# Position-biased attention in a four-layer network: query copies stored column by column, a preparation in smaller pieces, and a new order of the first loads and blocks

## The chip, the cores and the metric

The kernel runs on one core of a Trainium2 chip, in one launch. The metric is the time of one execution on the device, in microseconds; the kernel before has a median of 4787.96 us in three runs (4782.0 to 4789.18).

A core has these engines, named as the profile names them: PE (TensorE, matrix products; PEld is its load of the stationary operand), DVE (VectorE), ACT (ScalarE), POOL (GpSimd) and SP (SyncE, which here only issues DMAs). Each works through its own queue in order. Products land in PSUM (eight banks of 512 float32 on each of 128 partitions), all else lives in SBUF.

## The reference

The network has four layers on x of shape (2, 64, 64, 128): two images of 4096 tokens with 128 channels. Only layer 0 is touched by the change:

```python
# x = x + _L0_conv_ref(_gn(x), w_qkv, pos_emb_h, pos_emb_w)
qkv = jnp.einsum('bhwc,cd->bhwd', x, w_qkv)
q, k, v = jnp.split(qkv, [128, 256], axis=-1)      # 4 heads of 32, L = 4096 tokens
pos = relative_position_bias(q, pos_emb_h, pos_emb_w).reshape(B, nh, L, L)
scores = jnp.einsum('bnqd,bnkd->bnqk', q, k) * scale + pos
attn = jax.nn.softmax(scores, axis=-1)
out = jnp.einsum('bnqk,bnkd->bnqd', attn, v)
```

`_gn` is a group normalization over an image (32 groups of 4 channels). The bias `pos` of a query at (row, column) and a key at (row', column') is the query times an embedding of row' − row, plus the query times an embedding of column' − column. Layer 1 (a triangular product with gates), layer 2 (attention with squared scores, then a mixture of 64 experts) and layer 3 (attention, then a mixture of 8 experts) follow.

## The kernel before, in words

**Schedule.** The kernel is written with a tile framework: it gives every instruction a priority by its place in the program, and orders each engine's queue with a model of the times, so an instruction that is ready in that model can stand ahead of earlier ones that are not. Semaphores follow from the tiles. A pool gives each tag a number of buffers.

**Head of layer 0** (`Net.__init__`, `layer0`). Eight DMAs of 512 KB on SP's queue bring x into SBUF, four for each image. The weights (192 KB) and the two position tables (16 KB each) come on ACT's queue. Then the tables are transposed into `pe`, and a chain of small products (`gram`, `traces`, `tops`) makes bounds on the size of queries and keys. For each image, eight `group_block`s transpose 512 tokens at a time (line 113), take statistics (DVE, line 116) and copy the transposed block to `xT` (ACT, line 118); `group_stats` makes mean and scale of the groups; two instructions at line 395 normalize `xT` in halves. `lengths` squares `xT` (one half of each image on GpSimd, the other on ACT) and sums the squares by a product. From these `at_most` decides between `l0_bounded`, the path that is taken here, and a general one. The preparation of the first unit runs in between: 16 of its pieces ahead of that decision in the program, the rest behind it, and then the values of image 0 (`l0_values`).

**Main loop** (`l0_bounded`). A unit is one image, a pair of heads and half of the queries (2048): eight units. A unit has four blocks of 512 queries and, for each, 32 steps over 128 keys. In a step TensorE makes scores of both heads (line 615), ACT takes their exp (line 623), DVE multiplies by the column part `ew` of the bias, itself an exp (line 626), and TensorE adds up the weighted sum of the values two steps later (line 573). The row part of the bias is in the scores: the operands `qa` and `ka` carry it in 32 extra rows for each head. Eight units of 128 steps make 1024 steps.

**Preparation of a unit** (`l0_prepare`). It is a generator; the loop of the unit before takes one piece of it in every second step (64 slots a unit), ahead of which go the finishes of query blocks (`l0_finish`, three pieces each). Its parts are:
- queries: `projected` makes 2 x 512 of them in one PSUM tile; for each 512, `qa` gets 32 rows of either head by six copies on ACT and DVE (lines 677 to 687). Four of them also fill the rows that later hold the row bias with a copy of the queries, of which the column-bias products read every 64th, that is one column of the image;
- column bias: in each of four groups 16 products (`l0pw`, line 701) with a moving operand `qa[lo : lo + HD, :, y::S]`, for 32 columns y from row group 32 and for 32 from row group 96, into two PSUM tiles, partitions 0 to 63 of each; then two exps (line 712) write them to `ew`, and one DMA copies `ew` to the other 64 partitions;
- row bias: in each of four groups 16 products (`l0ph`, line 723) from row groups 0 and 64 into the two halves of one PSUM tile, and four copies (line 734);
- keys, where the half is the first: four pairs of 512 (`l0pk`) and 16 copies (lines 747, 748).

A float32 product takes two passes, so the profile counts two matmuls for each product in these lines.

## Time and profile before

| | |
|---|---|
| three runs | 4789.18, 4787.96, 4782.0 us |
| profiled execution | 4783.74 us, span 4781.9 us |
| mean granted TensorE clock | 0.963 |
| layer 0: head (to the first score product) | 0 to 87.4 us, PE busy 53.09 of its first 87 us, granted clock 0.80 |
| layer 0: main loop | 87 to 2088 us, PE busy 1962 of 2001, clock 1.00 |
| layer 1 and what follows | 2088 to 4782 us |

A line of the timeline gives the start and the length in us, engine, source line, operation, the tile written and those read, shapes and how many instructions were merged; in square brackets stands how long the engine was idle before and what ended that. A line of the waits gives who waited for whom, the total in us, how often, and the longest. A line of the chain gives start, length and what held the end at that time. Of merged matmuls the length reaches to the end of the last one, which overlaps the next group; distances between starts tell what TensorE spends.

### The profile page before, as it was taken

The numbers are of one execution on the slowest core, as the hardware profiler recorded it, in microseconds if no ns is written. First come the engines' busy times: TensorE is split into PE (matmuls) and PEld (weight loads), VectorE is DVE, ScalarE is ACT, GpSimd is POOL, SyncE is SP. The second block draws the span as 40 slices with busy tenths as digits, with TensorE's granted clock in tenths as the row PEclk, the third lists the DMA queues.
The fourth block names the chain that finished last, engine by engine and source line by source line (L and its number), as shares of the span: only waits on it lengthen the run. The fifth ranks groups of instructions, "written<-read, shape, count | busy, mean of one in ns | idle before, by whom it ended". The sixth has DMA issues, their size and how long they took to land.

```text
span 4781.9 us, 76270 instructions
## 1 busy us (share of the span) xinstructions
PE 4464.8 (93%) x32236; PEld 1739.6 (36%) x32236; DVE 2943.9 (62%) x4850; ACT 2697.7 (56%) x3157; POOL 945.6 (20%) x848
## 2 busy tenths in 40 slices
PE   6999999999999999977899999999967999999999
PEld 3333333333333333335323223222224444444444
DVE  5676767677766767766755657555554444444447
ACT  5666565656666665545666766676731443433326
POOL 1000000000000000004455555555521000000008
PEclk8999999999999999988999999999978999999999
DMA  1000000000000000000000000000034000000001
GB/s 47 10 1 10 1 10 1 10 1 1 10 1 10 1 13 1 1 5 21 6 1 1 1 1 1 1 1 1 1 109 181 1 0 0 0 1 0 0 1 36
DMA packets 42562, 60.16 MB, mean 13 GB/s; under 512 B 4224, under 2 KB 24928, under 8 KB 41568
## 3 DMA queue, kind: packets, MB, share of 16 engines
q1 hardware_dynamic: 40912, 54.34, 3.7%
q8 instruction: 257, 4.21, 0.4%
q10 hardware_dynamic: 1296, 0.82, 0.1%
q14 instruction: 97, 0.79, 0.1%
HBM read 42.56 MB, written 4.19 MB: 10 GB/s over the span
## 4 chain that ended last, share of the span: by engine, by line
PE 75%; DVE 11%; ACT 7%; issue 3%; POOL 2%; DMA 1%; SPq 0%; DVEq 0%; ACTq 0%; POOLq 0%
PE l0o L573 15%; PE l0sc L615 15%; PE scl L2126 9%; PE oTl L2085 9%; PE l2sc L1498 5%; PE l2pos L1245 5%; PE l2av L1544 3%; PE f3ex L2235 2%; DVE l2es L1518 2%; POOL l2es L1521 2%; ACT l0es L623 2%; ACT l2es L1529 1%; DVE l0es L626 1%; PE l0pw L701 1%; PE l1p L988 1%
## 5 line engine op out<-in xcount | busy, mean ns | idle before, releaser
L626 DVE TENSOR_TENSOR l0es<-l0es,l0qe 128x1024 f32<-128x1024 f32 x1024 | 1250.2, 1228 | 529.5 <-ACT l0es L623 528.4
L623 ACT ACTIVATE l0es<-l0sc 128x1024 f32<-128x1024 f32 x1024 | 1044.0, 1025 | 604.5 <-PE l0sc L615 599.5
L573 PE MATMUL l0o<-l0es,l0v 64*33 64x512 f32 x8192 | 1072.9, 592 | 32.2 <-DVE l0es L626 16.7
L615 PE MATMUL l0sc<-l0qe,ka 64*64 64x512 f32 x8192 | 1080.3, 595 | 5.7 <-ACT l0es L623 5.0
L1529 ACT ACTIVATE l2es<-l2es 128x1024 f32<-128x1024 f32 (+3 forms) x576 | 559.4, 984 | 264.8 <-POOL l2es L1521 257.7
L1521 POOL TENSOR_TENSOR l2es<-l2es 128x1024 f32<-128x1024 f32 (+3 forms) x352 | 581.2, 1662 | 493.6 <-DVE l2es L1518 424.9
L2093 DVE TENSOR_TENSOR accl<-accl,esl 128x1024 f32<-128x1024 f32 x240 | 302.5, 1261 | 424.6 <-ACT esl L2137 421.2
L1518 DVE TENSOR_SCALAR l2es<-l2sc 128x1024 f32<-128x1024 f32 (+3 forms) x320 | 338.8, 1059 | 312.1 <-PE l2sc L1498 311.5
L2137 ACT ACTIVATE esl<-scl 128x1024 f32<-128x1024 f32 x240 | 245.8, 1024 | 485.0 <-PE scl L2126 451.7
L615 PEld LDWEIGHTS l0sc<-l0qe,ka 64*64 64x64 f32 x8192 | 298.5, 133 | 568.0 <-issue 490.4
L573 PEld LDWEIGHTS l0o<-l0es,l0v 64*33 64x33 f32 x8192 | 255.5, 108 | 646.6 <-issue 518.7
L2126 PE MATMUL scl<-l3qT,l3kT 128*128 128x512 f32 x1024 | 487.3, 595 | 0.0
L1498 PE MATMUL l2sc<-l2q,kept 32*128 32x512 f32 (+3 forms) x2304 | 392.2, 624 | 86.2 <-ACT l2es L1509 62.2
L2085 PE MATMUL oTl<-esl,l3v 128*128 128x512 f32 x960 | 451.1, 592 | 0.0
L776 POOL TENSOR_TENSOR x<-x,l0y 128x256 f32<-128x256 f32 x32 | 23.4, 730 | 1994.5 <-DVE l0y L771 1899.8
L1544 PE MATMUL l2av<-l2es,kept 128*32 128x512 f32 (+3 forms) x2304 | 309.5, 588 | 0.0
L1245 PE MATMUL l2pos<-kept 128*32 128x512 f32 x2416 | 295.2, 597 | 0.1
L2085 PEld LDWEIGHTS oTl<-esl,l3v 128*128 128x128 f32 x960 | 181.7, 190 | 225.6 <-issue 221.8
L2126 PEld LDWEIGHTS scl<-l3qT,l3kT 128*128 128x128 f32 x1024 | 188.2, 191 | 207.5 <-issue 191.3
L1509 ACT ACTIVATE l2es<-l2sc 128x1024 f32<-128x1024 f32 x224 | 226.3, 1010 | 52.5 <-PE l2sc L1498 51.3
L1498 PEld LDWEIGHTS l2sc<-l2q,kept 32*128 32x128 f32 x2304 | 116.9, 188 | 329.4 <-ACT l2es L1509 163.5
L1245 PEld LDWEIGHTS l2pos<-kept 128*32 128x32 f32 x2416 | 78.1, 111 | 173.8 <-issue 173.0
(707 smaller groups left out, 3748.9 us busy)
## 6 DMA issues: line engine op xcount, KB each, us to landing
f2w<-in_L_ffn_weight_dram SPq DMA_DIRECT2D x32, 1024.0 KB, 13.1
l0qe<-l0qe SPq DMA_DIRECT2D x8, 1024.0 KB, 6.7
x<-in_x_dram SPq DMA_DIRECT2D x8, 512.0 KB, 8.8
out_dram<-x SPq DMA_DIRECT2D x16, 256.0 KB, 2.3
kept<-in_L_attn_pos_rev_dram SPq DMA_DIRECT2D x1, 1792.0 KB, 6.8
ew<-in_L_ffn_expert_w_dram SPq DMA_DIRECT2D x1, 512.0 KB, 4.1
kept<-in_L_attn_pos_rev_dram SPq DMA_DIRECT2D x1, 256.0 KB
f2b<-in_L_ffn_weight_dram ACTq DMA_DIRECT2D x2, 128.0 KB, 2.6
```

The lines of the kernel that those rows point to most:

```text
L573: nc.tensor.matmul(o[64 * h : 64 * h + HD + 1, r, :], lhsT=v1[rows, k, 2 * pair + h, :], rhs=es[rows, h, :], start=(k == 0), stop=(k == NC ...
L615: nc.tensor.matmul(sc[64 * c : 64 * c + 64, h, :], lhsT=ka[rows, k0 : k0 + 64], rhs=qa[rows, k // (NC // 2), qs], start=True, stop=True,)
L623: nc.scalar.activation(es, sc, AF.Exp)
L626: nc.vector.tensor_tensor(es, es, ew[:, :, qs], ALU.mult)
L1245: nc.tensor.matmul(out[part], lhsT=lhsT[:, part], rhs=rhs, start=start, stop=stop)
L1498: nc.tensor.matmul(sc[:, h2, off:], lhsT=kT[hs, k * P : (k + 1) * P], rhs=q[hs, off:], start=True, stop=True,)
L1518: nc.vector.tensor_scalar(es[:, :, lo:], sc[:, :, lo:], root, None, ALU.mult)
L1521: nc.gpsimd.tensor_tensor(part, part, part, ALU.mult)
L1529: nc.scalar.activation(es[:, :, off:], es[:, :, off:], AF.Silu)
L1544: nc.tensor.matmul(avs[i][hs, off:], lhsT=v[:, k, hs], rhs=es[h // 2][:, h % 2, off:], start=(k == 0), stop=last,)
L2085: nc.tensor.matmul(oT, lhsT=vs[b][:, k, :], rhs=es[:, i, :], start=(k == 0), stop=(k == NC - 1),)
L2126: nc.tensor.matmul(sc[:, i, :], lhsT=kTs[b][:, k * P : (k + 1) * P], rhs=qT[:, qb * 512 : (qb + 1) * 512], start=True, stop=True,)
```

## The change

- The position tables are loaded first on ACT's queue, then the weights, then blocks 4 and 5 of x (the first half of image 1); SP loads the other six.
- In the program the blocks and the normalization of image 0 and the blocks of image 1 now come first, then the tables and bounds, then image 1's normalization and the lengths; the whole preparation of the first unit comes behind the decision. Its PSUM tiles have a tag of their own (`first`, four buffers beside four of `misc`, in place of five).
- The square of the second half of image 1 is made on ACT and no longer on GpSimd.
- The queries for the column bias are written column by column, so that the 32 queries of a column lie together; the copies per 512 queries become eight, in three pieces.
- The column-bias products of both row groups go to the two halves of one PSUM tile.
- The two exps of a group, the two pairs of row-bias copies and the two pairs of key copies become pieces of their own.
- The copies of the values alternate between ACT and DVE.

The diff, cut to its core:

```diff
@@ __init__
-        src = ins["x"].rearrange("b h w c -> (b h w) c").rearrange("(g p) c -> p g c", p=P)
-        for g in range(0, B * NC, 8):
-            nc.sync.dma_start(out=self.x[:, g : g + 8, :], in_=src[:, g : g + 8, :])
+        self.load_x(nc.sync, [0, 1, 2, 3, 6, 7])
...
+    def load_x(self, queue, blocks):
+        src = self.ins["x"].rearrange("b h w c -> (b h w) c").rearrange("(g p) c -> p g c", p=P)
+        for g in blocks:
+            blk = slice(8 * g, 8 * g + 8)
+            queue.dma_start(out=self.x[:, blk, :], in_=src[:, blk, :])
@@ layer0
+            raw = wp.tile([2 * S - 1, 2, HD], F32, tag="raw", name="l0raw")
+            for i, n in enumerate("hw"):
+                nc.scalar.dma_start(out=raw[:, i, :], in_=ins[f"L0_conv_pos_emb_{n}"])
             nc.scalar.dma_start(out=w, in_=ins["L0_conv_w_qkv"])
+            self.load_x(nc.scalar, [4, 5])
...
-                tc.tile_pool(reuse_waits="tile", name="l0sp", bufs=5, space=PSUM) as ps,
+                tc.tile_pool(reuse_waits="tile", name="l0sp", bufs=4, space=PSUM) as ps,
             ):
+                def blocks(b):
+                    for g in range(NC // 4):
+                        self.group_block(ps, gst[:, b], b, g, xT[:, b, :])
+
+                def normed(b):
+                    gm, gr = self.group_stats(ps, gst[:, b], b)
+                    for half in range(2):
+                        part = xT[:, b, half * 2048 : (half + 1) * 2048]
+                        nc.vector.tensor_scalar(part, part, gm, gr, ALU.subtract, ALU.mult)
+
+                blocks(0)
+                normed(0)
+                blocks(1)
...
-                made = {}
-                first = self.l0_prepare(
-                    ps, (0, 0, 0), xT, w, pe, [ka], (qe[:, 0], qe[:, 1]), made
-                )
...
-                    if half:
+                    if half and b == 0:
                         nc.gpsimd.tensor_tensor(sq, part, part, ALU.mult)
...
-                for b in range(B):
-                    for g in range(NC // 4):
-                        self.group_block(ps, gst[:, b], b, g, xT[:, b, :])
-                    gm, gr = self.group_stats(ps, gst[:, b], b)
-                    for half in range(2):
-                        part = xT[:, b, half * 2048 : (half + 1) * 2048]
-                        nc.vector.tensor_scalar(part, part, gm, gr, ALU.subtract, ALU.mult)
+                normed(1)
                 for b in range(B):
                     for half in range(2):
-                        pieces(4)
                         lengths(b, half)
...
-                for _ in first:
+                for _ in self.l0_prepare(
+                    ps, (0, 0, 0), xT, w, pe, [ka], (qe[:, 0], qe[:, 1]), {}, tag="first"
+                ):
                     pass
-                self.l0_values(ps, 0, xT, w, v)
+                self.l0_values(ps, 0, xT, w, v, tag="first")
@@ l0_values
-            nc.scalar.copy(
+            (nc.vector.tensor_copy if g % 2 else nc.scalar.copy)(
@@ l0_prepare
-                left = [
-                    v.rearrange("p (x y) -> p x y", y=S)[:, :, : S // 2]
-                    for v in (qa[32:64, 0, cols], p0)
-                ]
                 yield
-                nc.scalar.copy(qa[:64, 1, cols], pq[64 * i : 64 * i + 64])
-                nc.vector.tensor_copy(qa[:HD, 0, cols], p0)
+                nc.scalar.copy(qa[:HD, 0, cols], p0)
+                nc.vector.tensor_copy(qa[64 : 64 + HD, 0, cols], p1)
                 yield
-                nc.vector.tensor_copy(left[0], left[1])
-                for h, p in ((0, p0), (1, p1)):
-                    right = [
-                        v.rearrange("p (x y) -> p x y", y=S)[:, :, S // 2 :]
-                        for v in (qa[96:128, h, cols], p)
-                    ]
-                    (nc.scalar.copy if h else nc.vector.tensor_copy)(right[0], right[1])
-                nc.scalar.copy(
-                    qa[64 : 64 + HD, :, cols], p1.unsqueeze(1).broadcast_to([HD, 2, 512])
-                )
+                nc.scalar.copy(qa[64 : 64 + HD, 1, cols], p1)
+                nc.vector.tensor_copy(qa[:HD, 1, cols], p0)
+                yield
+                for j in range(2):
+                    rows = slice(32 + 64 * j, 64 + 64 * j)
+                    for h, p, copy in ((0, p0, nc.scalar.copy), (1, p1, nc.vector.tensor_copy)):
+                        dst = qa[rows, h, : H2 // 2].rearrange("p (y x) -> p x y", y=S // 2)
+                        src = p.rearrange("p (x y) -> p x y", y=S)
+                        x = slice(8 * (g + i), 8 * (g + i) + 8)
+                        copy(dst[:, x, :], src[:, :, 32 * j : 32 * j + 32])
             yield
...
-            pw = [
-                ps.tile([P, 8, 2, S // 2], F32, tag="misc", name=f"l0pw{t}_{g}_{i}")
-                for i in range(2)
-            ]
+            pw = ps.tile([P, 8, 2, S // 2], F32, tag=tag, name=f"l0pw{t}_{g}")
...
-                        pw[i][:S, n, :, :],
+                        pw[64 * i : 64 * i + S, n, :, :],
                         lhsT=pe[lo : lo + HD, 1, S - 1 - y : 2 * S - 1 - y],
-                        rhs=qa[lo : lo + HD, :, y::S],
+                        rhs=qa[lo : lo + HD, :, (8 * g + n) * 32 : (8 * g + n + 1) * 32],
...
             for i in range(2):
+                if i:
+                    yield
                 y = 32 * i + 8 * g
                 dst = ew[:S].rearrange("p h (x y) -> p y h x", y=S)
-                nc.scalar.activation(dst[:, y : y + 8], pw[i][:S], AF.Exp)
+                nc.scalar.activation(dst[:, y : y + 8], pw[64 * i : 64 * i + S], AF.Exp)
...
             for lo in (0, 64):
+                if lo:
+                    yield
                 for kh, copy in ((0, nc.scalar.copy), (1, nc.vector.tensor_copy)):
...
                 pk = projected(1, g, f"l0pk{b}_{pair}_{g}")
-                yield
                 for i in range(2):
+                    yield
```

## The prediction

> **What bounds the kernel now.** I read the page first (shares, chain), then layer 0's stretches, its TensorE timeline, TensorE's waits, and the order of work in the first 90 us.
>
> ```profile
> span 4781.9 us, 76270 instructions
> PE 4464.8 (93%) x32236; PEld 1739.6 (36%) x32236; DVE 2943.9 (62%) x4850; ACT 2697.7 (56%) x3157; POOL 945.6 (20%) x848
> PE l0o L573 15%; PE l0sc L615 15%; PE scl L2126 9%; PE oTl L2085 9%; PE l2sc L1498 5%; PE l2pos L1245 5%; PE l2av L1544 3%; PE f3ex L2235 2%; DVE l2es L1518 2%; POOL l2es L1521 2%; ACT l0es L623 2%; ACT l2es L1529 1%; DVE l0es L626 1%; PE l0pw L701 1%; PE l1p L988 1%
> ```
>
> TensorE sets the end. Layer 0 runs from 0 to 2088 us: a head until the first score product at 87.41, then 1024 steps. Only layer 0 is edited, so the question is what TensorE does besides the steps, and how long the head is. TensorE's timeline in unit 0 shows the price of side work:
>
> ```profile
> 131.89 1.04 PE L573 MATMUL l0o<-l0es,l0v 64*33 64x512 f32 x8
> 132.86 1.98 PE L701 MATMUL l0pw<-l0qe,l0pe 32*64 32x64 f32 x32
> 134.76 1.09 PE L615 MATMUL l0sc<-l0qe,ka 64*64 64x512 f32 x8
> ...
> 178.32 1.04 PE L615 MATMUL l0sc<-l0qe,ka 64*64 64x512 f32 x8
> 179.18 1.04 PE L573 MATMUL l0o<-l0es,l0v 64*33 64x512 f32 x8
> 180.14 1.15 PE L723 MATMUL l0ph<-l0qe,l0pe 32*64 32x64 f32 x32
> 181.22 1.09 PE L615 MATMUL l0sc<-l0qe,ka 64*64 64x512 f32 x8
> ```
>
> The first column is the start. Groups of eight follow each other at 0.86 us (178.32 to 179.18), so a step is 1.72 us. A column-bias group (l0pw) holds TensorE from 131.89 + 0.86 = 132.75 to 134.76, 2.01 us; a row-bias group (l0ph), as many products of the same shape, from 180.04 to 181.22, 1.18 us.
>
> TensorE's waits from 90 to 2250 us, and one place behind the largest:
>
> ```profile
> PE l0o L573 <- DVE l0es L626: 16.7, 35, 2.3
> PE l0sc L615 <- ACT l0es L623: 5.0, 16, 1.9
> ```
> ```profile
> 352.06 0.58 ACT L677 COPY l0qe<-l0pq 64x512 f32<-64x512 f32 x1
> 352.66 1.02 ACT L623 ACTIVATE l0es<-l0sc 128x1024 f32<-128x1024 f32 x1
> 352.67 0.68 DVE L678 COPY l0qe<-l0pq 32x512 f32<-32x512 f32 x1 [0.81 <-ACT l0qe L677]
> ...
> 354.67 1.00 ACT L687 COPY l0qe<-l0pq 32x1024 f32<-32x1024 f32 x1
> 355.55 1.06 PE L573 MATMUL l0o<-l0es,l0v 64*33 64x512 f32 x8 [0.72 <-DVE l0es L626]
> ```
>
> The copies of queries sit ahead of exps and multiplications in the in-order queues, and the weighted sum comes late. Taking TensorE's groups from 352.65 to 358.03 against 0.86 each, this place loses 1.94 us. There are 14 such places (two in each of the seven units prepared in the loop); the same subtraction sums to 27.9 us.
>
> In the chain, the head starts like this:
>
> ```profile
> 1.94 11.20 DMA l0raw<-in_L_conv_pos_emb_w_dram
> 18.50 1.06 PE gt L113 x4
> 25.63 0.38 DVE gmv L125
> 34.03 1.81 DVE gst L116 x3
> 38.79 1.90 PE l0pq L657 x4
> 53.03 2.78 PE l0pw L701 x32
> ```
>
> TensorE's queue begins with the position table's transposes, which wait for a small DMA until 13.19; x's transposes queue behind and start at 18.43, when most of x has landed. The first query product stands behind image 1's statistics, at 38.72.
>
> **Column-bias products.** Before, the moving operand has a stride of 64 elements, and both row groups write the same 64 columns; after, it has runs of 32, and the groups write separate halves. L723's row has neither old trait: runs of 64, separate halves, 217 ns a product against 283 for L701. So I take 1.18 us: 2.01 − 1.18 = 0.83 us, 28 groups in the loop, 23.2 us, all on TensorE and so on the path. Bounds: 0 (both traits harmless, the weight load being the price: 148 ns against 133) and 25. The four groups in the head run at a granted clock of 0.50, where 64 pw products took 3.79 us and 122 ph ones 6.72: 59 against 55 ns, 0.5 us in all. One PSUM tile in place of two lets the next group start while the first is read; no wait on that shows today, so nothing.
>
> A page speaks against this edit: the Trainium skill, "PSUM — Partial Sum Buffer", section "PSUM bank collisions raise a hardware error", says that different row tiles cannot access one PSUM bank at the same time, and the new l0pw does just that. By it the pairs would not overlap, and the 23.2 us would be nothing. But l0ph puts row groups 0 and 64 into one tile's two halves and runs at 1.18 us: the row decides.
>
> **Query copies.** Of one 512-column block ACT did 0.58 + 0.36 + 1.00 = 1.95 us and DVE 0.68 + 0.42 + 0.42 = 1.52. After: each two copies of 512 (0.58; 0.69) and two of 256 whose writes step by 32 elements. ACT's strided exp (L712, 64x512 with step 64) takes 1.064 against 0.582 for the plain copy of that shape, 0.94 ns more an element, so ACT's 256 cost 0.36 to 0.60. On DVE the nearest strided row is L1058, 1.03 against 0.69 for 512, so 0.42 to 0.60. I take the strided ends: ACT 2.35, DVE 2.57 us a block; over 32 blocks (four a unit) that is 13 us more on ACT and 34 on DVE. Both engines have room: a step of 1.72 us holds 1.03 of exp and 1.23 of multiplication. What matters is how long one piece holds a queue. ACT's longest falls from 1.36 in a row (L686, L687) to about 1.2 with DVE turns between, in three pieces in place of two. The nearest row for such alternating pairs is L734 (0.58 on ACT, then 0.69 on DVE, twice a piece): around 180 to 186 TensorE loses nothing. Against it: ready pieces are pulled together (350.64 to 354.67), and DVE's 0.69 exceeds its free 0.49. So of 27.9 us lost I take 15 as regained, with bounds of −15 (losses half as large again) and 27.9 (as at L734).
>
> **The other pieces.** The exps of a group and the row-bias copies become two pieces each, the keys' copies too. Pieces per unit rise from 22 or 26 to 34 or 42; with about 12 of the finishes that is 54 at most of 64 slots, so none is left for the unit's end. They also put the SBUF copy on SP's queue later, with nothing behind it. PSUM copies of values alternate ACT (0.59) and DVE (0.69), while TensorE's 0.92 a group sets the pace: nothing.
>
> **Head.** Two loads of x move from SP's queue to ACT's, behind tables and weights. SP issued eight in 14.44 us, so two cost ACT's queue about 3.6 us; it has nothing else to do then, since x's first block must land. SP's later small loads start earlier and nobody waits. At 222 GB/s, with ACT's 1.2 MB sharing the engines, image 0 (2 MB) has landed by about (2 + 1.2) MB / 222 GB/s = 14.5 us, and TensorE now transposes block by block. Add two statistics (1.4) and today's path from aggregation to normalization (25.63 to 31.45, 5.8) and the first half of the normalization (1.3): query products at 23.0 in place of 38.7. From there to the first score is 87.4 − 38.7 = 48.7 us today. Into this falls more of image 1's work, and a square goes from GpSimd (3.60) to ACT (1.91); out go two table loads for a square root between exps (63.42, 65.69: 2.6 us), since no exp is issued that early any more. ACT was busy about 33 of those 48.7 us and TensorE about 35, so there are gaps to fill, and the second set of four PSUM tiles lets the preparation fill them. I take 46: first score at 69, a gain of 18. Bounds: 7, if image 1's statistics, normalization and copies (about 11 us) all lie on the path; 25, if copies fill ACT's gaps (23 + 39 us of ACT work).
>
> **Sum.** 23 + 0.5 + 15 + 18 = 56 us. The profiled execution took 4783.74 (span 4781.9, 1.8 around it), so 4727; the median of the runs is 4.2 higher, so I say 4731.
>
> **Rivals.**
> (a) Products and head gain, the copies' stalls stay, because pieces are pulled together again: 4788 − 42 = 4746. For it: 350.64 to 354.67.
> (b) Head gains nothing, because ACT, with its two loads, late copies and third square, sets its end: 4788 − 38 = 4750. For it: ACT's 8.64 busy of 10 us at 60 to 70; against: 5.68 and 6.62 in the windows before that.
> (c) The new layout does not do what it says, l0pw stays near 2 us: 4788 − 33 = 4755. For it: the weight loads; against: L723.
> (d) Slower. The alternation blocks both queues: eight hand-offs a block, DVE's copy waiting for ACT's and ACT's next for DVE's, each with exp or multiplication queued behind it and TensorE behind those. A place holds two blocks, 9.8 us of both engines' copies, of which 2.0 reach TensorE now. At 7 us it loses 14 × 5 = 70 more and the total is 4788 − 42 + 70 = 4816; it outweighs the products and the head from 2.0 + 42 / 14 = 5 us a place. For it: DVE waited for L677 27 times, 14.4 us; against: L734.
>
> **How the numbers follow.** Forecast 0.50 (4731; by its bounds from 4710, all at their best with 25 + 28 + 25, to 4753, with 23 + 5 + 7, below which it is one of the others), (a) 0.22, (b) 0.10, (c) 0.08, (d) 0.10. Reaching over (a), (b) and (c) and most of the forecast: 4706 to 4764. Runs of this kernel tell some 0.2% (9.6 us) from no change. Of (d)'s chance a little ends within that: faster 0.85, same 0.05, slower 0.10.
>
> **What would show it.** Right: l0pw's groups at about 1.2 us on TensorE, its matmul median near 217 ns; the first score product near 69 us and x's transposes from about 6; the wait of L573 for DVE's l0es well under 16.7 us. Wrong: l0pw still near 283 ns (c); a first score past 82 (b); waits for l0es above 25 us (a, then d). Outside layer 0 every stage should keep its length; a difference there would refute the working.

## The result: slower, and where the time went

The changed kernel took 4817.38 us in the median of four runs (4815.22 to 4823.44) beside 4787.91 for the kernel before: a ratio of 1.0066 with a 95% interval of 1.0049 to 1.0083. The forecast was 4731 with a range up to 4764. The profiled execution has a span of 4813.4 us, 31.5 more than before.

From the page of the changed kernel: the span, the engines' busy time, and the chain by line:

```profile
span 4813.4 us, 76320 instructions
PE 4468.1 (93%) x32236; PEld 1714.6 (36%) x32236; DVE 2984.2 (62%) x4890; ACT 2713.0 (56%) x3182; POOL 942.0 (20%) x847
PE l0o L577 15%; PE l0sc L619 15%; PE scl L2127 9%; PE oTl L2086 9%; PE l2sc L1499 5%; PE l2pos L1246 5%; PE l2av L1545 3%; PE f3ex L2236 2%; DVE l0es L630 2%; ACT l0es L627 2%; DVE l2es L1519 2%; POOL l2es L1522 2%; ACT l2es L1530 1%; PE l1p L989 1%; ACT l2es L1510 1%
```

TensorE still sets the end, and the column-bias products (1% of the chain before) are gone from this list. DVE's multiplications rose from 1% to 2%; ACT's exps stay at 2%. TensorE's waits from 90 to 2250 us (engine, line, what it waited for: us in total, times, longest) say which of the two holds it back:

```profile
PE l0sc L619 <- ACT l0es L627: 43.1, 26, 2.5
PE l0o L577 <- DVE l0es L630: 16.3, 26, 2.3
```

The second line is as before (16.7). The first was 5.0. The score products wait for a PSUM tile that the exp has not read yet, and the exp is late. The timeline of the changed kernel at the place that the prediction showed (start, us, engine, line):

```profile
349.74 1.02 ACT L627 ACTIVATE l0es<-l0sc 128x1024 f32<-128x1024 f32 x1
349.75 0.68 DVE L681 COPY l0qe<-l0pq 32x512 f32<-32x512 f32 x1 [0.64 <-ACT l0qe L680]
350.79 0.61 ACT L689 COPY l0qe<-l0pq 32x256 f32<-32x256 f32 x1
350.80 1.23 DVE L630 TENSOR_TENSOR l0es<-l0es,l0qe 128x1024 f32<-128x1024 f32 x1 [0.37 <-ACT l0es L627]
...
352.05 0.60 DVE L689 COPY l0qe<-l0pq 32x256 f32<-32x256 f32 x1
...
352.69 0.58 ACT L689 COPY l0qe<-l0pq 32x256 f32<-32x256 f32 x1 [1.29 <-DVE l0qe L689]
353.31 0.58 DVE L689 COPY l0qe<-l0pq 32x256 f32<-32x256 f32 x1 [0.65 <-ACT l0qe L689]
353.92 0.58 ACT L677 COPY l0qe<-l0pq 32x512 f32<-32x512 f32 x1 [0.65 <-DVE l0qe L689]
354.52 1.02 ACT L627 ACTIVATE l0es<-l0sc 128x1024 f32<-128x1024 f32 x1
354.53 0.70 DVE L678 COPY l0qe<-l0pq 32x512 f32<-32x512 f32 x1 [0.64 <-ACT l0qe L677]
...
355.60 1.09 PE L619 MATMUL l0sc<-l0qe,ka 64*64 64x512 f32 x8 [2.46 <-ACT l0es L627]
```

No two copies overlap: each waits until the other engine's has ended, and then for what stands ahead of it in its own queue. ACT's copy at 352.69 waited 1.29 us for DVE's, and that one stood behind a multiplication of 1.23 us. Between the exps at 349.74 and 354.52 lie 4.78 us where a step has 1.72. The block of 512 columns that follows (L677 at 353.92) starts without a gap behind the one before, and its first copy goes ahead of the late exp.

Beside that, the products themselves did what was forecast. TensorE's column-bias products in the loop (line, count: min/median/max ns):

```profile
L698 PE MATMUL l0pw<-l0qe,l0pe x896: 217/217/266, 148.2 to 1759.2; 32*64 32x64 f32 x180
```

For the account I take TensorE's groups of eight from the first score product to the end of layer 0's loop, and what each takes beyond 0.858 us until the next group. A place is the stretch in which query copies run, with 1 us ahead of it and 5 us behind. In us, from the traces (head: first score product):

| | before | changed | difference |
|---|---|---|---|
| head | 87.4 | 84.6 | −2.8 |
| column-bias products in the loop | 55.2 | 30.2 | −25.0 |
| lost at the 14 query places | 30.2 (2.0 a place, the first 5.0) | 78.4 (5.3) | +48.2 |
| lost elsewhere in the loop | 63.1 | 70.9 | +7.8 |
| behind the loop | 2694.0 | 2697.4 | +3.4 |

But for rounding these add up to the 31.5. So one term turned a gain into a loss, one gave almost nothing (2.8 of 18), and 8 us were not foreseen at all. The 3.4 behind the loop tell nothing: no kernel here changes what runs there, and that stretch spreads over 10.8 us in the traces of the 17 kernels.

### The profile page after: what moved, and what is told of

It is laid out like the page before. It is cut to its first block, busy times and chain, and to the rows that moved or that the text cites. A ratio compares the mean times of both kernels' runs of the same rounds, so it can differ in the third digit from the quotient of the medians.

```text
span 4813.4 us, 76320 instructions
## 1 busy us (share of the span) xinstructions
PE 4468.1 (93%) x32236; PEld 1714.6 (36%) x32236; DVE 2984.2 (62%) x4890; ACT 2713.0 (56%) x3182; POOL 942.0 (20%) x847
## 4 chain that ended last, share of the span: by engine, by line
PE 74%; DVE 11%; ACT 8%; issue 3%; POOL 3%; DMA 1%; SPq 0%; DVEq 0%; POOLq 0%; ACTq 0%
PE l0o L577 15%; PE l0sc L619 15%; PE scl L2127 9%; PE oTl L2086 9%; PE l2sc L1499 5%; PE l2pos L1246 5%; PE l2av L1545 3%; PE f3ex L2236 2%; DVE l0es L630 2%; ACT l0es L627 2%; DVE l2es L1519 2%; POOL l2es L1522 2%; ACT l2es L1530 1%; PE l1p L989 1%; ACT l2es L1510 1%
## 5 line engine op out<-in xcount | busy, mean ns | idle before, releaser
L619 PE MATMUL l0sc<-l0qe,ka 64*64 64x512 f32 x8192 | 1085.0, 598 | 43.3 <-ACT l0es L627 43.1
L619 PEld LDWEIGHTS l0sc<-l0qe,ka 64*64 64x64 f32 x8192 | 298.2, 133 | 608.5 <-issue 456.6
## 6 DMA issues: line engine op xcount, KB each, us to landing
x<-in_x_dram ACTq DMA_DIRECT2D x2, 512.0 KB, 10.8
```

Of the source, the lines that this page charges most:

```text
L619: nc.tensor.matmul(sc[64 * c : 64 * c + 64, h, :], lhsT=ka[rows, k0 : k0 + 64], rhs=qa[rows, k // (NC // 2), qs], start=True, stop=True,)
```

## Experiments

All start from the changed kernel; a time is the median, the ratio is to the kernel before in the same group of runs, with its 95% interval.

**What makes the query places dear.** Six kernels change the queries in the loop: their copies, and in some their products, tiles or storage.

`act_alone`: all eight copies on ACT, no turns.

```diff
+                act = nc.scalar.copy
+                dve = act if tag == "misc" else nc.vector.tensor_copy
...
-                nc.vector.tensor_copy(qa[64 : 64 + HD, 0, cols], p1)
+                dve(qa[64 : 64 + HD, 0, cols], p1)
...
```

> The changed kernel, but in the main loop all eight query copies of a 512-column block are made by ACT (the first unit's copies in the head stay shared). In the changed kernel TensorE loses 14 x 5.1 = 71 us behind the query copies. Theory (hand-offs: ACT and DVE read one PSUM tile in turns, each turn with an exp or a multiplication queued between): no turns are left, each ACT copy (0.58 to 0.60 us) fits the 0.69 us that a step leaves ACT, the loss falls below 15 us, the time to about 4760. Rival 1 (it is the amount of copy work, raised by the strided writes): one engine with all of it (4.7 us a block) loses as much or more, 4815 or above. Rival 2 (the finer pieces and new yields cost, not the copies): no change, 4810 to 4822.

Measured: 4830.2, 1.0085 (1.0068 to 1.0102); the places lose 97.7 us, 6.2 to 8.1 each. I had expected less than 15: one engine without turns is worse. Its copies are still one behind the other, and two exps then lie 5.8 us apart:

```profile
353.21 1.01 ACT L627 ACTIVATE l0es<-l0sc 128x1024 f32<-128x1024 f32 x1
354.24 2.47 ACT L691 COPY l0qe<-l0pq 32x256 f32<-32x256 f32 x4
...
359.03 1.02 ACT L627 ACTIVATE l0es<-l0sc 128x1024 f32<-128x1024 f32 x1
...
360.10 1.99 PE L619 MATMUL l0sc<-l0qe,ka 64*64 64x512 f32 x8 [3.51 <-ACT l0es L627]
```

`two_tiles`: each of the two 512-column blocks in a tile of its own, one copied by ACT, the other by DVE.

```diff
+                for i, copy in ((0, act), (1, dve)):
+                    out = ps.tile([P, 512], F32, tag=tag, name=f"l0pq{t}_{g + i}")
...
+                    own.append(list(placed(g, i, out[:32], out[32:64], (copy, copy))))
```

> The changed kernel, but in the main loop the queries of two 512-column blocks go to two PSUM tiles, one copied by ACT alone and one by DVE alone: the same copies in number, shape and share of each engine, and no turns. Theory (hand-offs): the loss falls from 71 to 10 to 30 us, 4760 to 4777; DVE's 0.69 us copies still exceed the 0.49 us that a step leaves it. Rival 1 (amount of copy work): within 5 us of the changed kernel. Rival 2 (finer pieces): no change.

Measured: 4790.2, 1.0008 (0.9998 to 1.0018); the places lose 43.2 (2.8 each), but the query products rise from 14.1 to 26.1. The same copies with the same writes, without turns: 35 us less are lost, though more than the 10 to 30 that I had expected. ACT's and DVE's copies now overlap, in long runs:

```profile
345.85 4.09 ACT L703 COPY l0qe<-l0pq 32x512 f32<-32x512 f32 x7 [0.81 <-PE l0pq L691]
346.71 3.29 DVE L703 COPY l0qe<-l0pq 32x512 f32<-32x512 f32 x5 [0.41 <-PE l0pq L691]
349.97 1.02 ACT L627 ACTIVATE l0es<-l0sc 128x1024 f32<-128x1024 f32 x1
```

`plain_writes`: the same copies, but no write steps (so the queries are not where the column-bias products look for them).

```diff
+                        if tag == "misc":
+                            dst = qa[rows, h, : H2 // 2].rearrange("p (x y) -> p x y", y=S // 2)
```

> The changed kernel, but in the main loop the four 256-element copies of a block write runs of 32 with no step between them. The column-bias products then read queries of other tokens, so the bias of seven units belongs to other queries. Theory (hand-offs): the turns stay and are only shorter, by 0.24 us on ACT and 0.18 on DVE for 56 copies each, 23 us of engine time of which about half shows: 4803 to 4810. Rival 1 (amount of work through strided writes): the loss falls from 71 to near the 28 us of the kernel before, 4775 to 4785. Rival 2: no change.

Measured: 4803.5, 1.0035 (1.0023 to 1.0048); 64.1 lost, 4.3 a place. The stepped writes are 14 of the 48 us, not the main part.

`old_copies`: in the loop the copies and the storage of the kernel before, and products that read with a step of 64; everything else as changed.

```diff
+                if tag == "misc":
...
+                    nc.scalar.copy(qa[:64, 1, cols], pq[64 * i : 64 * i + 64])
+                    nc.vector.tensor_copy(qa[:HD, 0, cols], p0)
...
+                        rhs=qa[lo : lo + HD, :, y::S]
+                        if tag == "misc"
+                        else qa[lo : lo + HD, :, (8 * g + n) * 32 : (8 * g + n + 1) * 32],
```

> The changed kernel, but in the main loop the query copies are those of the kernel before (six a block, queries kept in order of the tokens), so that the column-bias products read every 64th element again, while they still go to the two halves of one PSUM tile. All theories of the copies: the loss falls from 71 to about 28 us, -43. For the products it separates the two traits: if the step of 64 was what made them slow, a group takes 2.0 us again (+23), about 4797; if it was that both row groups wrote the same columns, it stays at 1.2, about 4774.

Measured: 4790.0, 1.0011 (1.0002 to 1.0021); the places lose 29.8, as before, and the column-bias products cost 53.5 again, though their groups still write two halves of one tile:

```profile
L718 PE MATMUL l0pw<-l0qe,l0pe x896: 281/283/302, 129.7 to 1720.9; 32*64 32x64 f32 x180
```

So the step of 64 in the moving operand was the slow trait. The 8 us elsewhere stay (70.7): they are not from the copies.

`chunk512`: a product, a tile and an engine for each head, block by block.

```diff
+            for c in range(0, H2, 512):
+                for h in range(2):
+                    out = ps.tile([P, 512], F32, tag=tag, name=f"l0pq{t}_{c}_{h}")
+                    nc.tensor.matmul(
+                        out[32 * h : 32 * h + 32, :512],
+                        lhsT=w[:, 64 * pair + 32 * h : 64 * pair + 32 * h + 32],
...
+                yield
+                for h, copy in ((0, nc.scalar.copy), (1, nc.vector.tensor_copy)):
+                    p = own[h]
...
```

> The changed kernel, but in the main loop each 512-column block of queries is projected by a product of its own, two slots apart, head 0 into one PSUM tile that only ACT reads (one copy of 2 x 512, 1.0 us, and two strided ones, 0.6 each) and head 1 into another that only DVE reads (about 1.2 and 2 x 0.6). Theory (a run of copies without an exp between them, lengthened by turns, delays exp and multiplication): runs of 2.2 and 2.4 us in place of four turns and two blocks together; the loss at the queries falls from 78 to about 25 to 35 us, the time to about 4770. Rival 1 (amount of copy work, which is nearly the same): no change, 4810 to 4822.

Measured: 4766.3, 0.9962 (0.9948 to 0.9976): faster than both. Most blocks lose 0.5, 16.3 in all. It also makes six copies of a block in place of eight, of nearly the same length in all (4.6 us beside 4.9). Its timeline shows the engines side by side:

```profile
349.85 1.00 ACT L687 COPY l0qe<-l0pq 32x1024 f32<-32x1024 f32 x1 [0.78 <-PE l0pq L676]
350.36 1.22 DVE L687 COPY l0qe<-l0pq 32x1024 f32<-32x1024 f32 x1
350.88 1.20 ACT L696 COPY l0qe<-l0pq 32x256 f32<-32x256 f32 x2
351.61 1.20 DVE L696 COPY l0qe<-l0pq 32x256 f32<-32x256 f32 x2
352.10 1.94 ACT L627 ACTIVATE l0es<-l0sc 128x1024 f32<-128x1024 f32 x2
```

`chunk256`: the same with 256 columns.

```diff
+            for c in range(0, H2, 256):
```

> As with 512, but in chunks of 256 columns, eight of them, two slots apart: runs of about 1.3 us on ACT and 1.5 on DVE between two exps or multiplications, with some 15% more engine time in all (twice as many instructions). Theory (length of a run without an exp): a run exceeds the free 0.69 and 0.49 us of a step by 0.6 and 1.0, which two buffers of scores and three of weights can hide; the loss falls below 10 us, the time to 4745 to 4755. Rival 1 (amount of work): no better than 512, or worse.

Measured: 4768.8, 0.9968 (0.9955 to 0.9980); at most of its 54 places the loss is 0.2, at one beside layer 1's work 11.0, and the query products cost 4.3 us more than with 512. The gain that I had expected of still shorter runs (4745 to 4755) did not come.

**Turns, or the length of what runs together?** `chunk512` and `two_tiles` leave three readings: hand-offs, the sum of copies, blocks that run together.

`old_division`: the new columns, copied with three hand-offs a block in place of eight.

```diff
-                nc.scalar.copy(qa[:HD, 0, cols], p0)
-                nc.vector.tensor_copy(qa[64 : 64 + HD, 0, cols], p1)
+                nc.scalar.copy(qa[:HD, 1, cols], p0)
+                nc.vector.tensor_copy(qa[:HD, 0, cols], p0)
...
+                nc.vector.tensor_copy(*half_of(slice(32, 64), 0, p0, 0))
+                nc.vector.tensor_copy(*half_of(slice(96, 128), 0, p0, 1))
+                nc.scalar.copy(*half_of(slice(32, 64), 1, p1, 0))
+                nc.scalar.copy(*half_of(slice(96, 128), 1, p1, 1))
+                nc.scalar.copy(
+                    qa[64 : 64 + HD, :, cols], p1.unsqueeze(1).broadcast_to([HD, 2, 512])
+                )
```

> The column storage stays, but the copies of a block are divided as the kernel before divides them: three in a row on VectorE (0.69 + 0.60 + 0.60 us), four on ScalarE (0.58 + 0.60 + 0.60 + 1.00), so that a block has three hand-offs in place of eight; the product and its tile stay as they are. My theory, that the turns on one tile make the loss: excess at the queries 2 to 3.5 us a place (30 to 50 in all, after: 78.4), column-bias products stay at 30.2, time 4770 to 4788. Rival one, that only the amount of copying counts (both engines' sum is as in the changed kernel): it stays near 78, time about 4817. Rival two, that ScalarE's 5.6 us of copies a place (the changed kernel: 4.7) are what delays the exps: over 78, as where ScalarE copied alone (97.7), time 4817 to 4830.

Measured: 4805.8, 1.0042 (1.0028 to 1.0055); 67.6 lost, 3.8 to 5.7 a place, the first 7.1 (its copies are divided so in the head too, which is 2.8 us shorter). I had expected 30 to 50: counting hand-offs is not enough. The copies are still one behind the other, and the second block follows at once:

```profile
349.03 1.00 ACT L690 COPY l0qe<-l0pq 32x1024 f32<-32x1024 f32 x1
...
350.06 0.58 ACT L683 COPY l0qe<-l0pq 32x512 f32<-32x512 f32 x1
350.66 1.02 ACT L627 ACTIVATE l0es<-l0sc 128x1024 f32<-128x1024 f32 x1
```

`one_block`: every copy and every turn kept, each block with a product of its own.

```diff
-        for g in range(0, H2 // 512, 2):
-            pq = projected(0, half * (H2 // 512) + g, f"l0pq{t}_{g}")
+        for g in range(H2 // 512):
+            at = (half * (H2 // 512) + g) * 512
+            pq = ps.tile([P, 512], F32, tag=tag, name=f"l0pq{t}_{g}")
+            nc.tensor.matmul(
+                pq[:64, :],
+                lhsT=w[:, 64 * pair : 64 * pair + 64],
+                rhs=xT[:, b, at : at + 512],
...
```

> All copies and all turns stay as in the changed kernel; only each 512-column block is projected by its own product into its own tile, so a place has 8 copies (4.9 us of both engines in series) in place of 16 (9.8 us). Theory A, that the copies of one tile run one after another and only what their sum exceeds some 4.5 us reaches TensorE (before 6.9 us of copies lose 2.0, old division 9.3 lose 4.8, after 9.8 lose 5.3): each of 28 places loses about 0.5 us, 10 to 20 in all (after: 78.4), the query products cost about 12 us more, time 4765 to 4780. Theory B, that every hand-off between the engines costs its share: the loss stays near 75, with the products' 12 the time is 4822 to 4830.

Measured: 4817.4, 1.0067 (1.0053 to 1.0081); 76.9 lost: most blocks 1.9, seven of 4.3 to 5.8. My theory A (the sum of copies beyond some 4.5 us) fell: 4.9 us of copies lose 1.9, not 0.5. Theory B's loss of 75 came, but not for its reason: at six of the seven dear blocks TensorE waited 2.6 to 3.0 us for ACT's copy of a finished query block (`l0os`), which here follows right behind the query copies. TensorE's waits for it, in the changed kernel and here:

```profile
PE l0o L577 <- ACT l0os L586: 10.6, 29, 0.5
PE l0o L577 <- ACT l0os L586: 28.4, 30, 3.0
```

With the stretches of the places twice as many, they also take in some of what counts as elsewhere: both together are 139.7 us here and 149.3 in the changed kernel. Before the wait at a typical block stands the same pair as in the changed kernel, a copy of DVE behind a multiplication and ACT's next copy behind it:

```profile
349.20 1.23 DVE L630 TENSOR_TENSOR l0es<-l0es,l0qe 128x1024 f32<-128x1024 f32 x1 [0.37 <-ACT l0es L627]
350.46 0.60 DVE L696 COPY l0qe<-l0pq 32x256 f32<-32x256 f32 x1
351.10 0.58 ACT L696 COPY l0qe<-l0pq 32x256 f32<-32x256 f32 x1 [1.29 <-DVE l0qe L696]
351.70 1.94 ACT L627 ACTIVATE l0es<-l0sc 128x1024 f32<-128x1024 f32 x2
352.78 1.09 PE L619 MATMUL l0sc<-l0qe,ka 64*64 64x512 f32 x8 [1.23 <-ACT l0es L627]
```

Loss for two blocks of 512 columns at a typical place, from the four runs:

| | two blocks at once | block by block |
|---|---|---|
| ACT and DVE on one tile | 5.3 (changed) | 2 × 1.9 (`one_block`) |
| a tile for each engine | 2.8 (`two_tiles`) | 2 × 0.5 (`chunk512`) |

At typical places both causes show, and the shared tile is the larger: 2.5 and 2.8 us (two blocks: 5.3 − 2.8; single: 3.8 − 1.0), the blocks together 1.5 and 1.8. The share of the blocks rests on these places alone; summed over all places it hardly shows (78.4 and 76.9), because of the seven dear blocks. What costs on a shared tile is that all its copies run one after another. How many hand-offs that takes does not decide (three a block in `old_division`, none in `act_alone`), and a rule that gives the loss from the sum was not found.

**The 8 us elsewhere.**

`row_whole` takes back the split of the row-bias copies.

```diff
             for lo in (0, 64):
-                if lo:
-                    yield
```

> Only the split of the row-bias copies into two pieces is undone. My theory, that the second pair of copies arrives a slot later and holds back the multiplication of the next step by 0.27 us at each of 28 places: the other excess falls from 70.9 to about 63, time 4809 to 4810. Rival, that the 8 us come from the shorter column-bias products before them, which give VectorE less time to clear its queue: it stays at 71, time 4817.

Measured: 4814.5, 1.0060 (1.0046 to 1.0073); 71.6 elsewhere. My theory fell. The rival's figure came, but the next run, where the products are as short and the 8 us are gone, refutes its reason.

`pw_two_tiles` takes back the one tile of the column-bias products.

```diff
-            pw = ps.tile([P, 8, 2, S // 2], F32, tag=tag, name=f"l0pw{t}_{g}")
+            pw = [
+                ps.tile([P, 8, 2, S // 2], F32, tag=tag, name=f"l0pw{t}_{g}_{i}")
+                for i in range(2)
+            ]
```

> Only the column-bias products go back to two PSUM tiles, each on partitions 0 to 63; the columns stay stored one after another. From one column-bias group's start to the start of the seventh score or weighted-sum group behind it, six times 0.858 us taken off, the kernel before loses 1.95 us, the changed one 1.43, and the bare products would be 1.1. My theory, that the two exps of a group overlap when they read two tiles (before: the next exp starts 1.76 us after the first of them, 2.16 in the changed kernel): 1.1 to 1.2 a place, other excess 62 to 65, time 4808 to 4811; the products keep 30.2 in all. Rival one, that the shorter products themselves uncover the exps: 1.43 stays, time 4817. Rival two, that the halves of one tile are what makes the products fast: they go back towards 55, time 4830 to 4842.

Measured: 4808.5, 1.0049 (1.0036 to 1.0063); 62.8 elsewhere: all of the 8 us, read from the traces (as times, this kernel's interval and the changed one's overlap). From a group's start to the seventh group behind it, less six times 0.858, it takes 1.13 us (before 1.95, changed 1.43). In the changed kernel the exps of one tile run one after the other, and the next exp starts 2.16 us behind the first:

```profile
172.77 2.13 ACT L711 ACTIVATE l0qe<-l0pw 64x512 f32<-64x512 f32 x2 [0.89 <-PE l0pw L698]
...
174.93 1.94 ACT L627 ACTIVATE l0es<-l0sc 128x1024 f32<-128x1024 f32 x2
177.26 1.06 PE L577 MATMUL l0o<-l0es,l0v 64*33 64x512 f32 x8
```

With two tiles they overlap by 0.2 us, as before:

```profile
169.75 1.93 ACT L714 ACTIVATE l0qe<-l0pw 64x512 f32<-64x512 f32 x2 [0.87 <-PE l0pw L701]
```

And the products are as quick in two tiles as in one (the same view as for the changed kernel): the tile's halves gave nothing, the columns gave all.

```profile
L701 PE MATMUL l0pw<-l0qe,l0pe x896: 216/217/267, 145.5 to 1748.5; 32*64 32x64 f32 x180
```

**The head.** Four kernels change only what comes before the loop.

`old_head`: the head of the kernel before (loads, order, the first unit's preparation in pieces); the loop as changed.

```diff
-        self.load_x(nc.sync, [0, 1, 2, 3, 6, 7])
+        self.load_x(nc.sync, range(8))
...
-                blocks(0)
-                normed(0)
-                blocks(1)
```

> The changed kernel's main loop and preparation with the head of the kernel before: all of x on SP's queue, tables and bounds first, 16 pieces of the preparation ahead of the decision. If the new order of the head gains what little it seems to (84.6 against 87.4 us), the first score product comes at 87 to 92 us and the time is 4820 to 4825. Rival (the new copies alone, with their turns, cost the head what the new order gained): 92 or later, since then the old order with the new copies pays both.

Measured: 4824.2, 1.0084 (1.0067 to 1.0101); first score at 90.0. With the same copies the new order thus gains 5.4 us of head (90.0 to 84.6); with the old order the new preparation loses 2.6 (87.4 to 90.0).

`first_halves`: `chunk512`'s copies in the head alone.

```diff
+        if tag == "first":
+            for c in range(0, H2, 512):
```

> The changed kernel, but only the first unit, in the head, has its queries copied from one PSUM tile for each engine (blocks of 512). The loop is the changed one, with its losses. Theory for the head (the copies, which last from 27.7 to 52.8 us, are held by turns between ACT and DVE, with image 1's statistics queued between): they end near 45 and the first score product moves from 84.6 to about 77, 4809. Rival (image 1's own chain and squares fill ACT and DVE anyway): 83 to 86, no change of the time.

Measured: 4812.0, 1.0062 (1.0045 to 1.0079); first score at 81.3. The copies end at 48.4, 4.4 us earlier, the first score 3.3: between my theory (77) and the rival (83 to 86). The squares of image 1 (51.30 to 55.0 on ACT) stand ahead of all but one of the exps of the column bias.

`unit_first`: the first unit's preparation is emitted behind image 0's normalization and the tables, ahead of image 1's blocks.

```diff
                 normed(0)
-                blocks(1)
...
+                for _ in self.l0_prepare(
+                    ps, (0, 0, 0), xT, w, pe, [ka], (qe[:, 0], qe[:, 1]), {}, tag="first"
+                ):
+                    pass
+                blocks(1)
```

> The first unit's preparation is emitted right behind image 0's normalization and the position tables, ahead of image 1's blocks; the loop is as in the changed kernel. My theory, that image 1's copies, statistics and squares in ScalarE's and VectorE's queues hold back the first unit's copies (52.85 in the changed kernel): these end at 37 to 42, column-bias products start by 43, and the first score product moves from 84.6 to 70 to 78, time 4803 to 4811; two more loads of ScalarE's tables (1.3 us each) are in that. Rival, that the bound on the scores (image 1's squares, which the branch waits for) sets the head's end: the copies end early, but the first score stays at 82 to 90, because all of image 1's work only comes later, time 4815 to 4823.

Measured: 4824.7, 1.0078 (1.0065 to 1.0092); column-bias products from 44.45, but the first score at 86.6. The rival held: what is put off comes later, and the branch waits for it.

`no_squares`: without image 0's and image 1's squares; the bound on the scores is then not the true one.

```diff
+                nc.vector.memset(most, 1.0)
...
-                for b in range(B):
-                    for half in range(2):
-                        lengths(b, half)
```

> Leaves out the squares of both images, their products and their maxima, and puts 1 in place of the maxima, so the bound on the scores is not the true one; everything else is as in the changed kernel. My theory, that these 5.7 us of ScalarE and 2.8 us of VectorE, with the products between, stand ahead of the first unit's copies in the same queues: the copies end at 45 to 48 in place of 52.85 and the first score product comes at 76 to 80 in place of 84.6, time 4808 to 4813. Rival, that image 1's statistics and the position tables hold the copies and the squares lie in gaps: the copies end past 51, the first score at 82 to 85, time 4815 to 4818.

Measured: 4810.0, 1.0049 (1.0033 to 1.0064); column-bias products from 47.69 (changed: 52.16), first score at 75.9, 8.7 earlier.

**All three mendings.** `both_mended`: `chunk512`'s copies in the loop and the head, and `pw_two_tiles`.

> Three parts together: one product, one tile and one engine for each head's query block, in the loop and in the head, and the column-bias products in two tiles; the rest is as in the changed kernel. If the parts add up: query places lose 16 in all, other excess 62 to 65, column-bias products 30.2, first score product at 79 to 82; against the loop with the mended query copies alone (4766.3) 8 us less in the loop and 3 to 5 in the head, time 4752 to 4758. If the exps of the column bias and the copies' places are not independent (the ScalarE time that one frees is taken by the other): time 4760 to 4767.

Measured: 4750.6 (4748.9 to 4755.4), 0.9926 (0.9913 to 0.9940): the fastest of all, a little under my 4752 to 4758. From its page:

```profile
span 4747.7 us, 76399 instructions
PE 4455.1 (94%) x32300; PEld 1714.9 (36%) x32300; DVE 2976.1 (63%) x4858; ACT 2700.4 (57%) x3150; POOL 943.8 (20%) x847
```

TensorE's waits from 80 to 2250 us:

```profile
PE l0o L577 <- DVE l0es L630: 15.7, 35, 3.3
```

That is the largest one for l0es; L619's wait for ACT's exps is no longer among the largest. Against before: column-bias products −25.0, query places −13.8 (30.2 to 16.4), query products +13.4, elsewhere −1.2, head −2.9, behind the loop −4.7 (within the spread said above); together −34.2, as the spans (4781.9 to 4747.7). The first score at 84.5 is later than in `first_halves` (81.3) or `pw_two_tiles` (81.9). The trace shows where: all exps of the column bias stand behind image 1's squares and begin at 56.04 (`first_halves`: 50.45), the column-bias products wait for them, and the row-bias products start at 63.57 in place of 59.03. What put the exps there was not tried.

## Why the prediction failed, step by step

**Column-bias products: right.** 23.2 us were forecast, 25.0 came, 217 ns a matmul as read from L723's row. The row could not say which trait counted; `old_copies` and `pw_two_tiles` say it was the step. The Trainium skill, "PSUM — Partial Sum Buffer", section "PSUM bank collisions raise a hardware error", quotes AWS that two row tiles may not use one bank at once. The prediction took this as a price on the one tile; none shows, it is 217 ns a matmul with one tile and with two. The sentence just ahead of it on the page, which the prediction left out, lets different column tiles use disjoint partitions of one bank at the same time, and the two halves are that as well; so the page need not speak against the edit. Rival (c) is out.

**Query copies: the step that failed.** "Of 27.9 us lost I take 15 as regained, with bounds of −15 (losses half as large again) and 27.9 (as at L734)": it was −48. Two choices made it. L734 was called the nearest row, but there four copies stand alone with a product of their own; here sixteen come together. And the sum of both engines' copies was split into 2.35 on ACT and 2.57 on DVE, as if they ran side by side, though the text quotes DVE L678 waiting 0.81 for ACT L677. In series they are 4.92 a block, with a multiplication of 1.23 in between. The lower bound should have come from that sum. The sizes of the copies were right: stepped writes took 0.58 to 0.61 on both engines, 0.60 forecast. Rival (d) named the mechanism. That its 4816 is so near the measured 4817.38 is luck: it had 7 us a place, which was 5.3, and counted the head's gain of 18, of which 2.8 came. The sign that the prediction set for the rivals (a) and (d), waits for l0es above 25 us, came with 59.4 (43.1 + 16.3).

The same section of that page says that the compiler puts an order between any two engines' accesses to one bank on the same 32 partitions, reads included. The turns here go further: in the tile's second block ACT's L677 (353.92) reads partitions 64 to 95 and DVE's L678 (354.53) reads 96 to 127, and DVE has waited 0.64 us for it. That the order comes from the shared tile, and not from `qa`, which both engines write, is shown by `chunk512`: there both engines write the same block of `qa` at the same time, from two tiles. Whether the tile or the bank is what is ordered, no run here tells.

**Other pieces at nothing: half right.** The split of the row-bias copies cost nothing (`row_whole`: 71.6 against 70.9). "One PSUM tile in place of two lets the next group start while the first is read; no wait on that shows today, so nothing" was wrong by 8 us: it looked at the tile's release, and not at the two exps that read it.

**Head: the first half came, the second did not; this step failed too.** x's transposes start at 6.31 and the query product at 25.8 (forecast 23.0). But "I take 46" for the way from there to the first score was 58.8. The timeline of the changed kernel shows the last copies in between image 1's work:

```profile
25.82 1.94 PE L661 MATMUL l0pq<-xT,wqkv 128*64 128x512 f32 x8 [0.34 <-DVE xT L295]
27.68 0.56 ACT L677 COPY l0qe<-l0pq 32x512 f32<-32x512 f32 x1
...
46.54 3.71 ACT L384 ACTIVATE l0sq<-xT 128x2048 f32<-128x2048 f32 x2 [1.68 <-DVE xT L295]
...
50.27 0.59 ACT L689 COPY l0qe<-l0pq 32x256 f32<-32x256 f32 x1
50.89 0.60 DVE L689 COPY l0qe<-l0pq 32x256 f32<-32x256 f32 x1 [2.48 <-ACT l0qe L689]
...
52.90 1.76 PE L698 MATMUL l0pw<-l0qe,l0pe 32*64 32x64 f32 x28 [0.26 <-DVE l0qe L689]
```

From the first copy (27.68) to the last (52.84) pass 25.2 us. A copy that waits for the other engine waits for all that stands in front of that copy: a square of ACT held up DVE's copy at 50.89 for 2.48 us. The gain at the start (15.7 by forecast, 38.7 to 23.0; 12.9 in fact) was down to 1.9 at the last copy, which ended at 54.77 before. The bound of 7 was for image 1's work lying on the path once, not at every turn. But the turns are not the whole cause: with the copies done 4.4 us earlier the first score came 3.3 earlier (`first_halves`), and with them done 6.9 earlier it came no earlier at all (86.6, `unit_first`), since the decision waits for image 1's work. The squares' part is shown (`no_squares`: 8.7 us); how the rest of the missing 15 us divides stays open.

## What to carry to other kernels

When two engines copy out of one PSUM tile, add their copies up in series, together with what stands in each queue between them, before saying how they fit into a step; give each engine a tile of its own, and each block a product of its own, where that costs less than the turns (here 13.4 us more of products). Here pieces that became ready together ran together, though they were emitted slots apart; a product of their own in TensorE's in-order queue kept them apart. And a trait that a fast row lacks is not yet the slow one: two kernels that take the traits back singly cost little.

## What the runs showed that was not expected

A moving operand of 64 float32 with a step of 64 elements took 283 ns a matmul against 217 ns in runs of 32, in one tile or two. Two exps that read the two halves of one tile do not overlap (2.13 us), two that read separate tiles do (1.93 us), worth 8 us over 28 groups; whether the tile or the upper partitions make it was not tried. Copies on one engine alone (`act_alone`) were the slowest of all copies tried in the loop, so that turns were not the worst choice, only a worse one than separate tiles.
